# LSTMs over single nodes: the output gate by seven half-size products, and the input sums of every LSTM on GpSimd

## The chip, the cores and the metric

The kernel runs on one core of one Trainium2 chip. The metric is the device time of one execution in microseconds (us). All arithmetic is float32.

## The reference, cut to what matters

A graph network of four layers works on `x` of 128 graphs x 64 nodes x 256 features. Each layer adds its result to `x`. Layers 0, 1 and 3 are not touched. Layer 2 makes two graph mixes and then, for window lengths p = 1 to 4, runs an LSTM over windows of p consecutive nodes and writes its last state over the last node of each window:

```
def step(carry, x_t):
    h, c = carry
    g = x_t @ Wih.T + h @ Whh.T + bias
    i, f, gg, o = jnp.split(g, 4, axis=-1)
    c = sigmoid(f) * c + sigmoid(i) * tanh(gg)
    h = sigmoid(o) * tanh(c)
for p in range(1, MAX_SKIP + 1):
    wins = h[:, :nw * p, :].reshape(Bv * nw, p, Hd)
    last = _lstm_last(Wih[p-1], Whh[p-1], bih[p-1], bhh[p-1], wins)
    h = h.at[:, arange(nw) * p + (p - 1), :].set(last)
```

The state starts at zero, so that for p = 1 (a window is a single node) there is one step, without `h @ Whh.T` and without the gate f: only i, g and o are computed.

## The kernel before

`windows` (line 2150) is the part that computes these LSTMs. The activations lie transposed, features on the 128 partitions in two halves of 128 (index `kc` or `k`), in four tiles `big`, one for every 32 graphs; `nodes(q)` views one as features x node x graph. For each p the windows are cut into chunks: 16 chunks of 16 windows for p = 1, 8 for p = 2, 8 of 10 or 11 windows for p = 3, and 4 of 16 windows for p = 4. Chunks go in pairs, and for every step t of a window `lstm` (line 2239) is called for both chunks of the pair in turn. That makes 72 calls: 16, 16, 24 and 16. A chunk has `W` = 16 x windows columns for each half of its 32 graphs: 256, or 160 and 176 for p = 3.

A gate is a product of a 256 x 256 weight and a 256 x 2W block, two by two blocks of each. Done directly, that is 8 products of 128 x 128 by 128 x W. `lstm` uses Strassen's scheme (in Winograd's form) with 7: sums of weight blocks are made once for each p in `weights` (S1 to S4), sums of the input blocks in each call. The latter stand in the tile `ls_tx`, of which there are two in rotation (`tp`, two buffers): three subtractions, first one of 512 columns (`T[:, 0:2]`), then two of 256 each that need the one before. From the second step on, the same sums of the state h (`S`) are made too, on VectorE.

`gates(xs, fs)` (line 2266) makes the gates `xs` of a call: first (0, 2), the gates i and g together, then o, alone at t = 0 and with f later. `product(m, bank, first)` issues the matmuls of product m for each gate in `xs`; the seven come in the order 1, 6, 7, 5, 2, 4, 3, of which 6, 7, 5 and 4 read `ls_tx`, and 1, 2 and 3 read the activations in `big`. Products of one sum share a PSUM bank, four banks ("a", "b", "f", "d") for each call of `gates`, out of seven in rotation (`lsps`). Around the products VectorE adds partial sums (tiles `ls_z`, `U` in a tile X, and the gate tile `ls_g`) and ScalarE copies (`ls_z`) and applies sigmoid or tanh with the bias. Then VectorE multiplies the gates into c (a tile X), ScalarE takes tanh of c, and VectorE writes the product into `big`.

For p = 1 the gate o is an exception before the change: it is made directly, in two halves of the output, each by two matmuls over 512 columns into one PSUM bank and one sigmoid that reads the bank.

The order of instructions on each engine is set by the framework's scheduler. The engines are called through a wrapper whose line is 799, so that nearly all instructions stand under L799 in the profile and are told apart by their tiles. A matmul in float32 leaves two records in the trace, and so does its weight load.

In the profile the weights of p = 1 and 3 lie in tiles called X, those of p = 2 and 4 in `ls_w` and `ls_s`. GpSimd has 26 instructions before the change, index tables and fills, none in the stage of the LSTMs.

Of the kernel before, what the change touches and what calls it, by code (L numbers as in the profile page):

```python
# [8 lines left out]
F32 = mybir.dt.float32  # L9
I32 = mybir.dt.int32  # L10
AF = mybir.ActivationFunctionType
ALU = mybir.AluOpType
# [1431 lines left out]
P = 128  # L1444
NB = 16
TPB = 4
BT = 512
# [18 lines left out]
class Kernel:  # L1466
# [683 lines left out]
    def windows(self):  # L2150

        nc, o, io = self.nc, self.o, self.io
        cx, (w, wq, gp, tp, zp, psum, pst) = self.stage([("lsw", 1), ("lswq", 1), ("lsg", 2), ("lst", 2), ("lsz", 2),
                                                         ("lsps", 7), ("lstps", 1)], "tile")
        with cx:
            bias = w.tile([P, 4, 8], F32, name="ls_b")
            bh = w.tile([P, 4, 8], F32, name="ls_bh")  # L2160
            with nc.allow_non_contiguous_dma("a few values"):
                nc.sync.dma_start(bias[:], io["L2_gnn_bih"].rearrange("q (k p) -> p q k", p=P))
                nc.sync.dma_start(bh[:], io["L2_gnn_bhh"].rearrange("q (k p) -> p q k", p=P))
            o.add(bias[:], bias[:], bh[:])
            flat = [x[:].rearrange("p t d -> p (t d)") for x in self.X]
            self.c_, self.h_, self.th_ = Ring(flat[12:15]), Ring(flat[8:10]), Ring(flat[10:12])
            self.u_ = Ring([flat[15][:, 0:512], flat[15][:, 512:1024]])
            self.lp = gp, tp, zp, psum, bias

            def load(ap, n, x):  # L2170

                if x is None:
                    return ([wq.tile([P, 4 * D], F32, name=f"ls_w{n}{kc}")[:] for kc in range(2)]
                            + [wq.tile([P, 2 * D], F32, name=f"ls_s{n}{i}")[:] for i in range(3)])
                return [flat[x], flat[x + 1], flat[x + 2][:, 0:512], flat[x + 2][:, 512:1024], flat[x + 3][:, 0:512],
                        flat[x + 3][:, 512:1024]]

            def weights(p):

                out = []  # L2180
                for n, m in enumerate(("Wih", "Whh") if p > 1 else ("Wih",)):
                    t = load(None, n, None if p % 2 == 0 else 4 - 4 * n)
                    ap = io[f"L2_gnn_{m}_t"][p - 1]
                    for kc in range(2):
                        nc.sync.dma_start(t[kc], ap[kc * P:(kc + 1) * P, :])
                    A = [[t[kc].rearrange("p (x k m) -> p x k m", k=2, m=P)[:, :, k, :] for kc in range(2)]
                         for k in range(2)]
                    S1, S2, S4 = (y.rearrange("p (x m) -> p x m", m=P) for y in t[2:5])
                    o.add(S1, A[1][0], A[1][1])
                    o.sub(S2, S1, A[0][0])  # L2190
                    o.sub(S4, A[0][1], S2)
                    S3 = t[5].rearrange("p (x m) -> p x m", m=P) if len(t) > 5 else A[1][0]
                    o.sub(S3, A[0][0], A[1][0])
                    out.append({1: A[0][0], 2: A[0][1], 3: S4, 4: A[1][1], 5: S1, 6: S2, 7: S3,
                                "A": A})
                return out

            ready = weights(1)
            for p in range(1, 5):
                Ws = ready  # L2200
                nw = N // p
                parts = -(-nw // 16)
                chunks = []
                for q in range(NG):
                    w0 = 0
                    for k in range(parts):
                        w1 = w0 + (nw - w0) // (parts - k)
                        chunks.append((q, w0, w1))
                        w0 = w1
                for n in range(0, len(chunks), 2):  # L2210
                    if n == 2 and p < 4:
                        ready = weights(p + 1)
                    if n == 2 and p == 4:
                        self.fetch(0, 8)
                        for i in range(8):
                            self.back(i, pst, "pt")
                    two = [dict(q=q, w0=w0, w1=w1) for q, w0, w1 in chunks[n:n + 2]]
                    for t in range(p):
                        for ch in two:
                            self.lstm(p, t, ch, Ws)  # L2220
            self.fetch(8, NB)
# [17 lines left out]
    def lstm(self, p, t, ch, Ws):  # L2239


        o = self.o
        gp, tp, zp, psum, bias = self.lp
        w0, w1, H = ch["w0"], ch["w1"], self.nodes(ch["q"])
        nw = w1 - w0
        W = nw * 16
        at = slice(t + p * w0, t + p * (w1 - 1) + 1, p)
        node = lambda kc: H[:, kc, at, :]
        half = lambda kc: node(kc).rearrange("p w (h b) -> p h w b", h=2)

        T = tp.tile([P, 4, 256], F32, name="ls_tx")[:, :, 0:W].rearrange("p n (w b) -> p n w b", b=16)
        o.sub(T[:, 0:2], H[:, :, at, 16:32], half(0))
        o.sub(T[:, 2], H[:, 1, at, 16:32], T[:, 0])
        o.sub(T[:, 3], H[:, 1, at, 0:16], T[:, 2])
        parts = [(Ws[0], {1: H[:, 0, at, 0:16], 2: H[:, 1, at, 0:16], 3: H[:, 1, at, 16:32],
                          5: T[:, 0], 7: T[:, 1], 6: T[:, 2], 4: T[:, 3]})]
        if t:
            h = ch["h"].rearrange("p (k h w) -> p k h w", k=2, h=2)
# [6 lines left out]

        def gates(xs, fs):
            G = gp.tile([P, 2, 1024], F32, name="ls_g")
            if p == 1 and len(xs) == 1:
                for k in range(2):
                    ps = psum.tile([P, BT], F32, name="ps")  # L2270
                    for kc in range(2):
                        self.mm(ps[:, 0:2 * W].rearrange("p (w b) -> p w b", b=32), Ws[0]["A"][k][kc][:, xs[0], :],
                                node(kc), kc == 0, kc == 1)
                    self.act(G[:, 0, 2 * W * k:2 * W * (k + 1)].rearrange("p (h w b) -> p h w b", h=2, b=16),
                             ps[:, 0:2 * W].rearrange("p (w h b) -> p h w b", h=2, b=16), fs[0],
                             bias=bias[:, p - 1, 2 * xs[0] + k:2 * xs[0] + k + 1])
                return G
            n = len(xs)
            V = G[:, 0:n, 0:4 * W].rearrange("p x (k h w) -> p x k h w", k=2, h=2)
            banks = {}  # L2280

            def product(m, bank, first):
                if first:
                    banks[bank] = psum.tile([P, 2, 256], F32, name="ps")
                for i, x in enumerate(xs):
                    for j, (A, Bm) in enumerate(parts):
                        out = banks[bank][:, i, 0:W]
                        if len(Bm[m].shape) == 3:
                            out = out.rearrange("p (w b) -> p w b", b=16)
                        self.nc.tensor.matmul(out, A[m][:, x, :], Bm[m], start=first and i == 0 and j == 0,  # L2290
                                              stop=i == n - 1 and j == len(parts) - 1, skip_group_check=True)
                return banks[bank][:, 0:n, 0:W]

            def b(x, k):
                return bias[:, p - 1, 2 * x + k:2 * x + k + 1]

            Z = zp.tile([P, 2, 256], F32, name="ls_z")[:, 0:n, 0:W]
            U = self.u_.next().rearrange("p (x w) -> p x w", x=2)[:, 0:n, 0:W]
            a = product(1, "a", True)
            self.act(Z, a, AF.Copy)  # L2300
            o.add(Z, Z, product(6, "b", True))
            o.add(U, Z, product(7, "f", True))
            o.add(V[:, :, 1, 1], U, product(5, "d", True))
            a = product(2, "a", False)
            for i, x in enumerate(xs):
                self.act(V[:, i, 0, 0], a[:, i], fs[i], bias=b(x, 0))
            o.add(V[:, :, 1, 0], Z, product(4, "f", False))
            for i, x in enumerate(xs):
                self.act(V[:, i, 1], V[:, i, 1], fs[i], bias=b(x, 1))
            o.add(V[:, :, 0, 1], Z, product(3, "d", False))  # L2310
            for i, x in enumerate(xs):
                self.act(V[:, i, 0, 1], V[:, i, 0, 1], fs[i], bias=b(x, 0))
            return G

        s = lambda g, i: g[:, i, 0:4 * W]
        G = gates((0, 2), (AF.Sigmoid, AF.Tanh))
        c = self.c_.next()[:, 0:4 * W]
        o.mul(c, s(G, 0), s(G, 1))
        if t:
            G = gates((3, 1), (AF.Sigmoid, AF.Sigmoid))  # L2320
            o.mul(s(G, 1), s(G, 1), ch["c"])
            o.add(c, c, s(G, 1))
        else:
            G = gates((3,), (AF.Sigmoid,))
# [334 lines left out]
```

## Time and profile before

| | |
|---|---|
| median of 3 runs | 2345.04 us (2342.6 to 2351.49) |
| profiled execution | 2348.6 us, its span 2346.8 us |
| mean granted TensorE clock | 0.993 |
| TensorE matmul busy | 2293.6 us (98%) |
| TensorE weight loads busy | 1629.2 us (69%), beside the matmuls |
| VectorE busy | 1602.6 us (68%) |
| ScalarE busy | 1134.3 us (48%) |
| GpSimd busy | 2.9 us |

Busy times are sums over the profiled execution. Instructions on one engine overlap a little at their ends, so that the distance of two starts is often less than the duration of the first. A view cut to a time window tells what each engine did in a stage; the LSTMs run from about 687 to 1757 us: p = 1 to 838 us, p = 2 to 1108 us, p = 3 to 1416 us, and p = 4 to the end.

### The profile page before, as it was taken

What the parts mean: (1) busy time and instruction counts of PE and PEld (TensorE: products, weight loads), DVE (VectorE), ACT (ScalarE), POOL (GpSimd) and SP (SyncE); (2) the same over time, 40 slices, a digit from 0 to 9 for tenths busy, and PEclk for the clock granted to TensorE, in tenths of its full rate; (3) what the DMA queues carried; (4) which work ended last, traced back from release to release, by engine and by line L of the source; (5) the groups of instructions that cost most, each with busy time, mean ns of one, the idle gap of its engine ahead of it and who ended that gap; (6) DMA issues with size and microseconds to landing.
All of it is one profiled execution on the core that took longest, in us unless ns stands there. A gap on an engine that the chain in (4) does not pass through costs nothing.

```text
span 2346.8 us, 32591 instructions
## 1 busy us (share of the span) xinstructions
PE 2293.6 (98%) x12153; PEld 1629.2 (69%) x12153; DVE 1602.6 (68%) x4006; ACT 1134.3 (48%) x2490; POOL 2.9 (0%) x26
## 2 busy tenths in 40 slices
PE   7999998999999999999999999999999999999989
PEld 4555446986777788888999998888874444444434
DVE  7877676998447777666777667569655566556467
ACT  5665864654436654444444434347445544344321
POOL 0000000000000000000000000000000000000000
PEclk9999999999999999999999999999999999999989
DMA  5000221230010000001000001000020000000001
GB/s 170 1 2 19 64 63 27 73 82 19 1 36 1 1 19 1 1 1 37 1 1 1 1 14 59 1 1 17 1 72 1 1 10 14 14 19 14 15 14 50
DMA packets 61192, 54.86 MB, mean 23 GB/s; under 512 B 15203, under 2 KB 58852, under 8 KB 61028
## 3 DMA queue, kind: packets, MB, share of 16 engines
q1 hardware_dynamic: 61028, 52.73, 7.3%
q8 instruction: 96, 1.57, 0.3%
q14 instruction: 68, 0.56, 0.1%
HBM read 35.93 MB, written 16.78 MB: 22 GB/s over the span
## 4 chain that ended last, share of the span: by engine, by line
PE 80%; DVE 3%; issue 0%; ACT 0%; ACTq 0%; DVEq 0%
PE ps L799 69%; PE acc L799 5%; PE pt L799 4%; PE pe L799 1%; DVE sm_m L799 1%; PE y L799 1%; DVE X L799 1%; DVE aw L799 0%; ACT ls_g L799 0%; DVE ls_g L799 0%; DVE sm_e L799 0%; DVE ls_t L799 0%; DVE XV L799 0%; DVE y L799 0%; DVE n_st L799 0%
## 5 line engine op out<-in xcount | busy, mean ns | idle before, releaser
L799 ACT ACTIVATE ls_g<-ls_g,ls_b 128x512 f32<-128x512 f32 (+4 forms) x472 | 242.9, 565 | 153.2 <-DVE ls_g L799 151.4
L799 ACT ACTIVATE ls_g<-ps,ls_b 128x256 f32<-128x256 f32 (+3 forms) x268 | 115.3, 470 | 330.6 <-PE ps L799 327.3
L799 PE MATMUL ps<-z,w 128*128 128x512 f32 x512 | 259.1, 630 | 0.9 <-ACT z L799 0.9
L799 PE MATMUL ps<-big,X 128*128 128x176 f32 (+3 forms) x848 | 212.9, 366 | 0.8 <-ACT big L799 0.7
L799 DVE TENSOR_TENSOR aw<-at,ed_OST 128x1024 f32<-128x1024 f32 x128 | 150.0, 1220 | 92.7 <-PE ps L799 92.7
L799 DVE TENSOR_TENSOR ls_g<-ls_z,ps 128x512 f32<-128x512 f32 (+5 forms) x256 | 146.9, 579 | 91.4 <-PE ps L799 90.0
L799 PE MATMUL ps<-ls_tx,X 128*128 128x160 f32 (+2 forms) x960 | 207.0, 326 | 0.6 <-ACT ls_g L799 0.6
L799 PE MATMUL ps<-X,X 128*128 128x160 f32 (+1 forms) x896 | 199.1, 306 | 0.0
L799 PE MATMUL ps<-X,ls_w 128*128 128x256 f32 x640 | 190.5, 379 | 0.0
L799 PEld LDWEIGHTS ps<-ls_tx,X 128*128 128x128 f32 x960 | 161.8, 190 | 15.4 <-DVE X L799 5.2
L799 PEld LDWEIGHTS ps<-big,X 128*128 128x128 f32 x848 | 145.9, 190 | 30.6 <-issue 19.4
L799 DVE TENSOR_TENSOR X<-ls_g 128x1024 f32<-128x1024 f32 (+2 forms) x108 | 117.4, 1087 | 51.1 <-ACT ls_g L799 51.1
L799 ACT ACTIVATE r<-ps 128x512 f32<-128x512 f32 x256 | 129.3, 625 | 41.4 <-PE ps L799 41.3
L799 PEld LDWEIGHTS ps<-X,X 128*128 128x128 f32 x896 | 148.4, 190 | 0.0
L799 PE MATMUL ps<-X,ls_s 128*128 128x256 f32 x480 | 142.3, 379 | 0.0
L799 PEld LDWEIGHTS ps<-z,w 128*128 128x128 f32 x512 | 88.8, 193 | 71.1 <-issue 62.6
L799 PE MATMUL ps<-ls_tx,ls_s 128*128 128x256 f32 x464 | 134.7, 379 | 0.0
L799 PE MATMUL ps<-ls_tx,ls_w 128*128 128x256 f32 x464 | 133.3, 380 | 0.0
L799 PEld LDWEIGHTS ps<-X,ls_w 128*128 128x128 f32 x640 | 121.4, 190 | 16.8 <-DVE X L799 0.3
L799 PE MATMUL ps<-big,ls_w 128*128 128x256 f32 x464 | 131.9, 379 | 0.7 <-ACT ls_z L799 0.7
L799 PE MATMUL ps<-ed_S,Q 64*128 64x512 f32 x512 | 128.3, 617 | 0.9 <-DVE XV L799 0.9
L799 ACT ACTIVATE h<-X,n_m,n_r 128x256 f32<-128x256 f32 x192 | 99.6, 589 | 40.9 <-issue 25.0
(532 smaller groups left out, 4012.0 us busy)
## 6 DMA issues: line engine op xcount, KB each, us to landing
X<-in_x_dram SPq DMA_DIRECT2D x32, 512.0 KB
xs<-X SPq DMA_DIRECT2D x16, 512.0 KB
X<-xs SPq DMA_DIRECT2D x16, 512.0 KB
out_dram<-X SPq DMA_DIRECT2D x32, 256.0 KB
X<-in_L_gnn_Wih_t_dram SPq DMA_DIRECT2D x4, 512.0 KB
ls_w<-in_L_gnn_Wih_t_dram SPq DMA_DIRECT2D x4, 512.0 KB
ls_w<-in_L_gnn_Whh_t_dram SPq DMA_DIRECT2D x4, 512.0 KB
w<-in_L_gnn_W_t_dram SPq DMA_DIRECT2D x2, 512.0 KB
```

Of the source, the lines that this page charges most:

```text
L799: i = method(*a, **kw)
```

## The change

For p = 1 the gate o goes through the same seven products as the others (`n` = 1 gate), and the direct form is gone; the weights no longer carry the plain blocks "A" for it. In all 72 calls the three subtractions into `ls_tx` are issued on GpSimd, and not through the ordered wrapper. The sums of the state h stay on VectorE.

```
-                    out.append({1: A[0][0], 2: A[0][1], 3: S4, 4: A[1][1], 5: S1, 6: S2, 7: S3,
-                                "A": A})
+                    out.append({1: A[0][0], 2: A[0][1], 3: S4, 4: A[1][1], 5: S1, 6: S2, 7: S3})
...
         T = tp.tile([P, 4, 256], F32, name="ls_tx")[:, :, 0:W].rearrange("p n (w b) -> p n w b", b=16)
-        o.sub(T[:, 0:2], H[:, :, at, 16:32], half(0))
-        o.sub(T[:, 2], H[:, 1, at, 16:32], T[:, 0])
-        o.sub(T[:, 3], H[:, 1, at, 0:16], T[:, 2])
+        less = lambda y, a, b: self.nc.gpsimd.tensor_tensor(y, a, b, op=ALU.subtract)
+        less(T[:, 0:2], H[:, :, at, 16:32], half(0))
+        less(T[:, 2], H[:, 1, at, 16:32], T[:, 0])
+        less(T[:, 3], H[:, 1, at, 0:16], T[:, 2])
...
         def gates(xs, fs):
             G = gp.tile([P, 2, 1024], F32, name="ls_g")
-            if p == 1 and len(xs) == 1:
-                for k in range(2):
-                    ps = psum.tile([P, BT], F32, name="ps")
-                    for kc in range(2):
-                        self.mm(ps[:, 0:2 * W].rearrange("p (w b) -> p w b", b=32), Ws[0]["A"][k][kc][:, xs[0], :],
-                                node(kc), kc == 0, kc == 1)
-                    self.act(G[:, 0, 2 * W * k:2 * W * (k + 1)].rearrange("p (h w b) -> p h w b", h=2, b=16),
-                             ps[:, 0:2 * W].rearrange("p (w h b) -> p h w b", h=2, b=16), fs[0],
-                             bias=bias[:, p - 1, 2 * xs[0] + k:2 * xs[0] + k + 1])
-                return G
             n = len(xs)
```

## The prediction

> **What bounds the kernel now.** I read the page's busy times first, then the stages of the LSTMs cut to windows, then the order in time of one chunk of p = 1, and last the groups by shape and the list of waits. The window table has, for each stretch, the stretch's length and the busy time of TensorE, its weight loads, VectorE, ScalarE and GpSimd:
>
> ```profile
> 687.00:838.50 151.50, 151.50 (x576) 109.32 (x577) 115.59 (x181) 92.28 (x160) 0.00 (x0) 1.00 0.02 8
> 838.50:1108.00 269.50, 269.50 (x1255) 236.24 (x1254) 182.72 (x294) 118.11 (x220) 0.00 (x0) 1.00 0.04 12
> 1108.00:1416.00 308.00, 307.26 (x2129) 304.38 (x2128) 215.99 (x458) 140.97 (x336) 0.00 (x0) 1.00 0.04 11
> 1416.00:1757.00 341.00, 338.87 (x1579) 291.64 (x1578) 232.95 (x424) 158.78 (x270) 0.00 (x0) 1.00 0.06 18
> ```
>
> TensorE is busy without a break in p = 1 and 2 and idle for 0.74 and 2.13 us in p = 3 and 4, at the full granted clock (1.00). A busy TensorE is not yet one at its pace, so the starts of its records must show that. One chunk of p = 1 in order of time, TensorE rows, then VectorE rows (start, length, row, and in brackets idle time before):
>
> ```profile
> 754.29 2.75 PE L799 MATMUL ps<-ls_tx,X 128*128 128x256 f32 x12
> 756.88 1.89 PE L799 MATMUL ps<-big,X 128*128 128x256 f32 x6
> 758.60 1.03 PE L799 MATMUL ps<-ls_tx,X 128*128 128x256 f32 x4
> 759.47 4.46 PE L799 MATMUL ps<-big,X 128*128 128x256 f32 x14
> 763.77 0.59 PE L799 MATMUL ps<-ls_tx,X 128*128 128x256 f32 x2
> ...
> 753.65 1.23 DVE L799 TENSOR_TENSOR X<-ls_g 128x1024 f32<-128x1024 f32 x1 [0.77 <-ACT ls_g L799]
> 755.43 0.69 DVE L799 TENSOR_TENSOR ls_z<-ls_z,ps 128x512 f32<-128x512 f32 x1 [0.55 <-PE ps L799]
> ...
> 759.67 0.69 DVE L799 TENSOR_TENSOR ls_g<-ls_z,ps 128x512 f32<-128x512 f32 x1 [0.92 <-PE ps L799]
> 760.27 0.69 DVE L799 TENSOR_TENSOR ls_tx<-big 128x512 f32<-128x512 f32 x1
> 760.88 0.68 DVE L799 TENSOR_TENSOR ls_g<-ls_z,ps 128x512 f32<-128x512 f32 x1
> 761.47 0.88 DVE L799 TENSOR_TENSOR ls_tx<-big,ls_tx 128x256 f32<-128x256 f32 x2
> 763.13 1.23 DVE L799 TENSOR_TENSOR X<-ls_g 128x1024 f32<-128x1024 f32 x1 [0.78 <-ACT ls_g L799]
> ```
>
> The first twelve records, all of 256 columns, take 756.88 - 754.29 = 2.59 us, 0.216 us each, with no gap to the next row. The chunk repeats after 763.77 - 754.29 = 9.48 us and has 576/16 = 36 records: 28 of 256 columns (14 matmuls of the gates i and g, two records each) and 8 of 512 (the gate o; the rows name only the first shape). So a record of 512 takes (9.48 - 28 x 0.216)/8 = 0.429 us. These are paces from start to start, and TensorE holds them through p = 1: it sets the time of this stage, and everything else lies beside it. In the same chunk VectorE is idle for 0.55 + 0.10 + 0.92 + 0.78 = 2.35 us (the 0.10 between rows left out here). In the list of waits TensorE waits for another engine six times in the 1070 us of the LSTMs, for 3.2 us in all.
>
> **Part 1: the gate o by seven products.** It takes out 4 matmuls of 512 columns (8 records) in each of the 16 chunks and puts in 7 of 256 (14 records); the order of instructions of the built programs agrees: 48 more matmuls, 3 for each chunk. A chunk goes from 9.48 us to 42 x 0.216 = 9.07 us: 0.41 us less, 16 times, **-6.6 us**. The weight loads rise from 36 to 42 of 0.190 us, 8.0 us in 9.07, still covered. These are the gains on the path, and small because one eighth of the products of one gate in three is saved, in a stage that is 6% of the span.
>
> What it adds beside the path: five VectorE additions of 256 columns in each chunk (before, sigmoid read the bank directly), and on ScalarE two sigmoids of 512 columns from PSUM become one copy and four sigmoids. p = 2 already has calls of just this form at t = 0 (o alone, seven products), so their cost stands in the trace:
>
> ```profile
> 846.50 0.41 DVE L799 TENSOR_TENSOR X<-ls_z,ps 128x256 f32<-128x256 f32 x1
> 846.83 0.68 DVE L799 TENSOR_TENSOR X<-X,X 128x512 f32<-128x512 f32 x1
> 847.43 0.41 DVE L799 TENSOR_TENSOR ls_g<-X,ps 128x256 f32<-128x256 f32 x1
> ```
>
> 0.33 us from start to start where the next is ready, 0.41 us by itself: five take 1.65 to 2.05 us. ScalarE goes from 92.28/16 = 5.8 us a chunk, by about 0.4 + 0.5 + 0.7 + 2 x 0.5 us less 2 x 0.68, to about 6.8 of 9.07. Its waits are not at their limit. The o gate now takes four PSUM banks where it took two, so eight banks of seven in rotation pass in each chunk. The calls of p = 2 at t = 0 pass the same eight, with more on VectorE, and TensorE is busy all through them; I cost this at nothing. If VectorE lagged by more than the bank rotation covers, the next product 1 or 6 would wait for a bank.
>
> **Part 2: the input sums on GpSimd.** VectorE loses 0.61 + 0.88 = 1.49 us in a chunk of p = 1. Its work there goes from 9.48 - 2.35 = 7.13 us to 7.13 - 1.49 + 1.65 to 2.05 = 7.3 to 7.7 us, of 9.07: still not the bound, with 1.4 to 1.8 us spare. Without the move it would be 8.8 to 9.2 us, the chunk itself.
>
> GpSimd makes no such subtraction in this trace. The nearest rows are
>
> ```profile
> L2353 POOL IOTA ed_J<- 128x512 f32 x1 | 0.6, 563 | 374.5 <-DVE bn_sh L799 374.5
> ...
> masks.py:199 POOL TENSOR_SCALAR_AFFINE_SELECT ident<-ident 128x128 f32<-128x128 f32 x1 | 0.3, 297 | 0.0
> ```
>
> Iota only writes: 0.56 us for 512 columns, and half for 256, gives 1.1 us a call, a lower end. The select reads one tensor; less 0.09 us, the cost of GpSimd's one-column fills, it takes 0.205 us for 128 columns, 1.6 ns a column: 0.91 + 2 x 0.50 = 1.9 us a call. Two tensors read in turn would double the slope: 1.73 + 2 x 0.91 = 3.6 us, the upper end. I take 1.9, the only row that reads at all.
>
> Is it on the path? A new wait stands at product 6, for GpSimd in place of VectorE. A tile of sums is free when product 4 of o of the call before last is done; by the order of instructions all 42 records of the other chunk and product 1 (4 records) stand between that and product 6. So GpSimd has 46 x 0.216 = 9.9 us for 1.9 (1.1 to 3.6) at p = 1, and 46 x 0.136 = 6.3 us for smaller sums in the shortest calls of p = 3. Nothing else is queued on GpSimd behind a sum but later sums; the first two can be made when the first activations are final, near 567 us, 120 us before TensorE needs them. Cost: nothing, up to 9.9 us a call.
>
> What the lighter VectorE gives back: between 680 and 1765 us the starts of TensorE's records exceed their paces (0.216, 0.149, 0.136 us by shape), counting single steps more than 30% over, by 9.3 us in all, of which 2.1 at the start of p = 3 (1108 to 1118 us) and 3.3 in p = 4 while finished blocks are turned back (1580 to 1611 us). In and just before these stretches input sums take 1.7 and 2.6 us of VectorE. The rest of the chain there (ScalarE, products into X) stays, so I take a third, **-1.4 us**, of bounds 0 and -9.3.
>
> **The rule against it.** VectorE instructions with two operands in SBUF are 1.23 + 1.29 = 2.5 us of a chunk (c, and the two products into `big`); the additions read PSUM. This trace has no moment where GpSimd reads beside them. The Trainium skill's page "SBUF — State Buffer", section "Who interferes with whom", says that a VectorE instruction with two SBUF inputs contends with a GpSimd instruction that reads SBUF: whichever starts first holds the shared port for its whole length. Its page "GPSIMD Engine Reference", section "Elementwise — side-by-side cycle accounting", keeps VectorE as the rule for elementwise work and gives 4497 ns for a 2048-column addition on GpSimd; my estimate from that is 1.1 + 2 x 0.55 = 2.2 us a call. By the two rules at their worst, every GpSimd instruction holding up VectorE in full, a chunk would be 7.3 to 7.7 + 2.2 = 9.5 to 9.9 us of VectorE, and the p = 1 stage would lose 7 to 13 us of what it gains.
>
> **Sum.** -6.6 - 1.4 = -8.0 us. The profiled execution was 2348.6 us (span 2346.8), 3.6 us above the median of the runs: 2340.6 us against it, **2337.0 us** against the median of 2345.0, or 0.34% less. What is late next is still TensorE.
>
> **Rivals.**
> (a) *VectorE becomes the bound of p = 1 because GpSimd's reads hold up its two-operand instructions.* Three such instructions meet three sums a chunk. With 1.9 us all blocked, VectorE needs 9.2 to 9.6 us: 0.1 to 0.5 us too much, 2 to 8 us in 16 chunks, 2339 to 2345. With 3.6 us all blocked, 10.9 to 11.3 us: 29 to 36 us lost, 2366 to 2373, slower than before. It turns from gain to loss when a chunk is held up 1.8 to 2.2 us in all. Against: they must collide every time, and PSUM's seven banks let VectorE lag. In p = 2 to 4 VectorE is at 68 to 70% with sums of its own, and the loss has room.
> (b) *GpSimd is far slower than its rows say on these strided reads, and the sums come late.* From 9.9 us a call, each us more costs up to 16 us in p = 1 alone. At 12 us: +34, 2371. Nothing in the profile speaks for it but the lack of a row.
> (c) *VectorE was late more often than I credit*: with 5 to 9.3 us of relief the sum is -11.6 to -15.9, 2329 to 2333.
>
> **How the numbers follow.** Half a per cent, 11.7 us, is about what a measurement of this kernel can tell from no change (its three runs spread over 9 us). My forecast, paced by TensorE throughout, 2333 to 2342, gets 0.74; (a) 0.12, of which 0.07 over half a per cent slower; (b) 0.03; (c) 0.11. The range leaves out the far end of (a) and (b) and of (c): 2330 to 2349. Within half a per cent 0.79, faster 0.11, slower 0.10.
>
> **What would show it.** Right: in p = 1 the chunk repeats every 9.07 us with 42 records at 0.216, the stage is near 145 us, GpSimd shows 216 subtractions of about 0.9 and 0.5 us, the waits of TensorE for GpSimd are empty, VectorE's idle time in p = 1 shrinks to 1 to 2 us a chunk, and the later stages keep their lengths within 2 us. Wrong: VectorE's products into X or `big` longer than 1.23 and 0.65 us or starting late while GpSimd runs (a), rows of TensorE waiting for `ls_tx` on POOL (b), or stages p = 3 and 4 shorter by more than 4 us (c).

## The result: 0.31% slower, and the profile after

Over 20 runs of each kernel the median went from 2347.72 to 2354.74 us; the ratio is 1.0031, 95% interval 1.0023 to 1.0039, which is 5 to 9 us slower where 8 us less were forecast. The profiled execution took 2354.23 us, its span 2352.3. The same two stretches of time that were shown of before, now of after:

```profile
687.00:838.50 151.50, 144.61 (x645) 119.05 (x644) 128.36 (x204) 95.05 (x182) 54.94 (x45) 1.00 0.01 4
838.50:1108.00 269.50, 268.57 (x1233) 232.26 (x1232) 169.23 (x251) 118.37 (x220) 50.67 (x48) 1.00 0.02 6
```

TensorE now idles for 6.9 us in a stretch in which it had no idle time. The stages are measured from the first product on `ls_tx` to the first matmul with the weights of p = 2, from there to the first product on `ls_tx` of p = 3, to the first matmul with the weights of p = 4, and to the last product on `ls_tx`. So measured p = 1 takes 157.2 us (before 150.9), p = 2 269.8 (266.9), p = 3 306.3 (306.0) and p = 4 334.5 (334.8). The parts of the program whose code is the same, ahead and behind, were 1.5 and 2.3 us shorter in this execution; in the runs below p = 1 begins anywhere between 681.6 and 690.2 us, so those two say nothing of the change. The loss is in p = 1, and a little in p = 2.

Two neighbouring chunks of p = 1 after the change, rows of TensorE, GpSimd and VectorE from the order in time (start, length, row, idle time before):

```profile
763.77 1.28 POOL L2251 TENSOR_TENSOR ls_tx<-big 128x512 f32<-128x512 f32 x1 [5.94 <-PE ps L799]
...
764.06 2.08 DVE L799 TENSOR_TENSOR X<-ls_g 128x1024 f32<-128x1024 f32 x1
...
765.13 2.41 POOL L2251 TENSOR_TENSOR ls_tx<-big,ls_tx 128x256 f32<-128x256 f32 x2
...
767.34 1.36 DVE L799 TENSOR_TENSOR big<-ls_g 128x512 f32<-128x512 f32 x2 [0.27 <-ACT ls_g L799]
...
767.50 1.46 PE L799 MATMUL ps<-big,X 128*128 128x256 f32 x6
...
768.62 0.67 DVE L799 TENSOR_TENSOR X<-ls_z,ps 128x512 f32<-128x512 f32 x1
...
769.43 1.10 PE L799 MATMUL ps<-ls_tx,X 128*128 128x256 f32 x4 [0.47 <-DVE X L799]
...
773.46 1.23 DVE L799 TENSOR_TENSOR X<-ls_g 128x1024 f32<-128x1024 f32 x1
...
773.82 2.02 POOL L2251 TENSOR_TENSOR ls_tx<-big 128x512 f32<-128x512 f32 x1 [6.27 <-PE ps L799]
...
775.91 1.54 POOL L2251 TENSOR_TENSOR ls_tx<-big,ls_tx 128x256 f32<-128x256 f32 x2
...
776.85 1.75 DVE L799 TENSOR_TENSOR big<-ls_g 128x512 f32<-128x512 f32 x2 [1.49 <-ACT ls_g L799]
```

In the first chunk GpSimd's long subtraction starts at 763.77, VectorE's product into c 0.29 us later, and c takes 2.08 us where it took 1.23. In the second, c starts first (773.46) and keeps its 1.23 us; now it is GpSimd's subtraction, 0.36 us later, that takes 2.02 and not 1.28. Then the sums run on beside the products into `big`, which take 1.75 in place of 1.29. Whoever comes first goes through, the other waits. The Trainium skill's page "SBUF — State Buffer", section "Who interferes with whom", states that a VectorE instruction with two SBUF inputs contends with a GpSimd instruction that reads SBUF, and that the order of issue decides who blocks; this trace agrees, with these numbers. The additions with one operand in PSUM keep their 0.67 to 0.69 us. GpSimd's start is not by chance: its tile of sums is released by the o gate's last product that reads it, just when c is due. So the engines meet in every chunk between 730 and 830 us: in every second one c takes 2.07 or 2.08 us, in the others GpSimd's long subtraction takes 1.95 to 2.02 us and the products into `big` are held up.

A chunk takes 10.01 us, averaged over ten (9.48 before, 9.07 forecast). The second TensorE row (769.43) is where TensorE feels it: product 4 (`ls_tx` x4) waits for VectorE's addition U (`X<-ls_z,ps`, 768.62). In the list of TensorE's waits over all LSTMs (us in total, times, longest) that is a line which was not there before:

```profile
PE ps L799 <- DVE X L799: 7.7, 15, 0.8
```

### The profile page after: what moved, and what is told of

Same layout as the page of the kernel before. It is cut to its first block, busy times and chain, and to the rows that moved or that the text cites. A ratio compares the mean times of both kernels' runs of the same rounds, so it can differ in the third digit from the quotient of the medians.

```text
span 2352.3 us, 33109 instructions
## 1 busy us (share of the span) xinstructions
PE 2289.9 (97%) x12249; PEld 1642.1 (70%) x12249; DVE 1569.6 (67%) x3870; ACT 1141.6 (49%) x2522; POOL 210.1 (9%) x242
## 4 chain that ended last, share of the span: by engine, by line
PE 75%; DVE 6%; ACT 1%; issue 1%; DMA 0%; DVEq 0%; ACTq 0%
PE ps L799 65%; PE acc L799 5%; PE pt L799 4%; DVE X L799 2%; ACT ls_g L799 1%; PE pe L799 1%; DVE sm_m L799 1%; DVE big L799 1%; PE y L799 1%; DVE ls_g L799 1%; DVE aw L799 0%; DVE ls_z L799 0%; DVE sm_e L799 0%; DMA ls_w<-in_L_gnn_Wih_t_dram 0%; DVE ls_s L799 0%
## 5 line engine op out<-in xcount | busy, mean ns | idle before, releaser
L799 ACT ACTIVATE ls_g<-ls_g,ls_b 128x512 f32<-128x512 f32 (+4 forms) x504 | 259.6, 567 | 149.3 <-DVE ls_g L799 146.8
L799 DVE TENSOR_TENSOR ls_g<-ls_z,ps 128x512 f32<-128x512 f32 (+5 forms) x288 | 159.2, 562 | 187.9 <-PE ps L799 187.7
L799 ACT ACTIVATE ls_g<-ps,ls_b 128x256 f32<-128x256 f32 (+2 forms) x252 | 101.0, 442 | 317.5 <-PE ps L799 314.8
L799 PE MATMUL ps<-ls_tx,X 128*128 128x256 f32 (+2 forms) x1088 | 244.1, 335 | 8.1 <-DVE X L799 7.4
L799 PEld LDWEIGHTS ps<-ls_tx,X 128*128 128x128 f32 x1088 | 183.9, 190 | 27.5 <-issue 12.1
L2251 POOL TENSOR_TENSOR ls_tx<-big 128x512 f32<-128x512 f32 (+1 forms) x72 | 99.6, 1384 | 1112.5 <-PE ps L799 912.9
L799 PE MATMUL ps<-big,X 128*128 128x256 f32 (+2 forms) x816 | 184.8, 333 | 0.7 <-ACT big L799 0.7
L799 DVE TENSOR_TENSOR X<-ls_g 128x1024 f32<-128x1024 f32 (+2 forms) x108 | 129.0, 1195 | 47.5 <-ACT ls_g L799 46.6
L799 PEld LDWEIGHTS ps<-big,X 128*128 128x128 f32 x816 | 139.1, 190 | 10.6 <-DVE ls_g L799 1.9
```

Source lines behind the costliest of these rows:

```text
L799: i = method(*a, **kw)
L2251: less = lambda y, a, b: self.nc.gpsimd.tensor_tensor(y, a, b, op=ALU.subtract)
```

## The experiments

Chunk times below are the mean of ten chunks in the middle of p = 1, from the starts of TensorE's records; "held up" is what c and the two products into `big` take beyond 1.22 and 2 x 0.69 us in a chunk. A ratio is the time against the kernel before, run beside it, with its 95% interval in brackets.

**The two halves, the reads taken away, and a bank of its own.** First each part of the change alone:

```
o_alone:     -        less = lambda y, a, b: self.nc.gpsimd.tensor_tensor(y, a, b, op=ALU.subtract)
             +        less = o.sub
sums_alone:  before.py with the three subtractions through `less` on GpSimd, nothing else
```

> The gate o of p = 1 by seven products, the input sums left on VectorE. Theory A (GpSimd's reads hold up VectorE's two-operand instructions, and that lateness reaches TensorE through product 4): without GpSimd p = 1 runs near TensorE's pace, 145 to 147 us where the change has 157, and the whole is 3 to 7 us below the kernel before. Theory B (the seven-product form of o alone makes the loop through VectorE and ScalarE longer than 9.07 us a chunk): p = 1 stays at 155 to 160 us and the whole is 5 to 9 us above before.

Measured: ratio 0.9982 (0.9971 to 0.9994), p = 1 147.8 us, 9.15 us a chunk. The seven products do pay, if little (1.4 to 6.8 us by the interval), VectorE has room for the sums, and theory B is out.

> The input sums on GpSimd in all calls, o of p = 1 direct as before. Theory A: the product into c and the products into the activations last 1.5 to 1.6 us and 0.8 us in p = 1 in place of 1.23 and 0.65; of the some 0.7 us a chunk a part shows, because the direct o leaves more room: p = 1 151 to 158 us, the whole 0 to 7 us above before. Theory B: p = 1 151 us, the whole within 2 us of before.

Measured: ratio 1.0006 (0.9996 to 1.0016); p = 1 151.6 us, and nothing held up: c 1.225, `big` 0.689 us, GpSimd's subtractions 1.29 and 0.73. The groups by shape between 730 and 830 us have

```profile
L799 DVE TENSOR_TENSOR X<-ls_g 128x1024 f32<-128x1024 f32 x10 | 12.3, 1225 | 13.4 <-ACT ls_g L799 13.4
L2252 POOL TENSOR_TENSOR ls_tx<-big,ls_tx 128x256 f32<-128x256 f32 x20 | 14.7, 733 | 1.6
L2252 POOL TENSOR_TENSOR ls_tx<-big 128x512 f32<-128x512 f32 x11 | 14.1, 1286 | 72.2 <-PE ps L799 72.2
```

With the direct o the sums happen to run while VectorE adds from PSUM (in one chunk from 772.04 to 774.95 us; c starts at 774.88). My expectation of a hold-up was wrong, and the point is a useful one: it is the meeting that costs, not the sums. p = 2 took 269.4 us, as in the change.

```
write_only:  +        def less(y, a, b):
             +            self.nc.gpsimd.memset(y, 0.0)
             +            self.nc.gpsimd.memset(y, 1.0)
own_bank:    -            o.add(V[:, :, 1, 0], Z, product(4, "f", False))
             +            o.add(V[:, :, 1, 0], U, product(4, "e", True))      # for p == 1
```

> The change with each of GpSimd's subtractions replaced by two fills of the same columns (the input sums are left out, the products take constants in their place): GpSimd writes the same tiles behind the same waits and reads nothing. Theory A: no hold-up, VectorE's product into c back at 1.23 us, p = 1 near 145 us, the whole 6 to 9 us below before. Theory B: p = 1 near 157 us as in the change, the whole about 7 us above before.

Measured: ratio 0.9969 (0.9956 to 0.9983), p = 1 147.4 us, 9.32 us a chunk. The groups by shape between 730 and 830 us, first of the change, then of this kernel:

```profile
L799 DVE TENSOR_TENSOR X<-ls_g 128x1024 f32<-128x1024 f32 x10 | 16.5, 1650 | 0.0
L2251 POOL TENSOR_TENSOR ls_tx<-big 128x512 f32<-128x512 f32 x10 | 16.4, 1639 | 61.8 <-PE ps L799 49.1 <-ACT ls_g L799 12.7
L799 DVE TENSOR_TENSOR big<-ls_g 128x512 f32<-128x512 f32 x20 | 15.9, 835 | 7.4 <-ACT ls_g L799 7.4
```

```profile
L799 DVE TENSOR_TENSOR X<-ls_g 128x1024 f32<-128x1024 f32 x11 | 13.4, 1222 | 0.0
L799 DVE TENSOR_TENSOR big<-ls_g 128x512 f32<-128x512 f32 x20 | 12.9, 689 | 5.4 <-ACT ls_g L799 5.4
L2252 POOL MEMSET ls_tx<- 128x512 f32 x11 | 5.8, 525 | 79.2 <-PE ps L799 79.2
```

The same tiles written on GpSimd, behind the same waits, hold nothing up: c is back at 1.22 and `big` at 0.69 us. With the kernel later_sums below, whose reads stay and are only moved, this shows that the cost is in reads that meet c and `big`. (The fills, 2 x 0.53 + 4 x 0.31 = 2.3 us a chunk, are a little shorter than the undisturbed subtractions, 2.75.)

> The change, but in p = 1 product 4 goes to a PSUM bank of its own and is added to U (Z plus product 7) and not to Z, so that it no longer waits for VectorE to have read product 7 out of the bank they shared; the sums are equal. Theories A and B alike, if product 4 is the place where the lateness reaches TensorE: p = 1 145 to 148 us, the whole 3 to 8 us below before. If VectorE is simply out of time, or the banks run out (ten pass in a chunk, of seven): 155 us or more, as the change.

Measured: ratio 1.0030 (1.0018 to 1.0041), p = 1 157.8 us, 9.94 us a chunk, held up 0.54 (all of it at `big`). The expectation of 145 to 148 us failed. Product 4 no longer waits for U, and nothing is won: TensorE's weight loads wait instead for VectorE's writes of `ls_g`. The list of waits between 700 and 835 us has

```profile
PEld ps L799 <- DVE ls_g L799: 15.1, 26, 0.9
```

The place where the lateness arrives can be moved; it did not go away.

**Another phase, and dose.** These kept the change and moved or scaled GpSimd's reads:

```
later_sums:  +            if len(self.past) > 2:      # p == 1; self.past: node(1) of each call
             +                self.nc.gpsimd.tensor_copy(T[:, 0, 0, 0:1], self.past[-3][:, 15, 31:32])
sums_twice:  each subtraction of p = 1 issued twice
p1_vector:   +        if p == 1: less = o.sub
p1_gpsimd:   +        if p > 1: less = o.sub
```

> The change, but in p = 1 each call's sums on GpSimd begin with a copy of one column out of the activations that the call before last wrote (into the tile of sums, overwritten at once by the first subtraction), so that they start behind VectorE's products into the activations, some 4.8 us later in the chunk, where VectorE has only additions that read PSUM. Order on the other engines as in the change. Theory A with the collision as its cause: product into c at 1.23 us and into the activations at 0.69 us, p = 1 146 to 149 us in place of 157, the whole 4 to 8 us below the kernel before. If the sums on GpSimd were costly for another reason (their own length, or a later tile), p = 1 stays at 155 us or grows.

Measured: ratio 1.0006 (0.9995 to 1.0017), p = 1 150.6 us, 9.42 us a chunk. Between 730 and 830 us:

```profile
L2255 POOL TENSOR_TENSOR ls_tx<-big 128x512 f32<-128x512 f32 x11 | 14.8, 1349 | 2.9 <-PE ps L799 2.1
L799 DVE TENSOR_TENSOR big<-ls_g 128x512 f32<-128x512 f32 x21 | 13.6, 688 | 7.3 <-ACT ls_g L799 7.2
L799 DVE TENSOR_TENSOR X<-ls_g 128x1024 f32<-128x1024 f32 x11 | 13.4, 1222 | 0.0
```

The same reads, started behind the products into `big`: nothing is held up, and 0.59 of the 0.94 us a chunk that the change loses against 9.07 are back. The gain over before that I expected did not come, for two reasons: 9.42 is not 9.07, and p = 2, with 269.7 us, keeps its loss.

> The change with each of the three subtractions of p = 1 issued twice on GpSimd, the second over the first. Theory A: GpSimd reads for twice as long, some 5.5 to 6 us of a chunk, and meets c and both products into the activations in every chunk: c 1.6 to 2.1 us, those 0.9 to 1.1 us each, p = 1 160 to 172 us in place of 157. Theory B: GpSimd's length does not matter as long as the sums are in time (9.9 us): 157 us.

Measured: 2364.6 us in one run, p = 1 164.6 us, 10.49 a chunk; c 1.65 and `big` 1.08 us, held up 1.20. TensorE also waited for the sums themselves here (12.3 us of weight loads between 730 and 830), so part of it is lateness of the tile, and the row of this kernel in the table below counts for less.

> The change with the input sums of p = 1 back on VectorE, those of p = 2 to 4 on GpSimd. Theory A: p = 1 as in the kernel with the gate o alone, 147 to 149 us; p = 2 stays at 269 to 270 us if what it lost (266.9 to 269.8) is GpSimd's reads in its own calls, and returns to 267 if it was handed on by p = 1; p = 3 and 4 306 and 334.5.

> The change with the input sums on GpSimd in p = 1 alone, those of p = 2 to 4 on VectorE. Theory A: p = 1 157 us as in the change; p = 2 back at 267 us if its own GpSimd reads cost the 2 to 3 us, 269 to 270 if p = 1 hands them on.

Measured, one run each: p1_vector 2345.59 us, p = 1 148.4 and p = 2 269.9; p1_gpsimd 2352.81 us, p = 1 156.9 and p = 2 267.0. The 2.9 us of p = 2 come from GpSimd's sums in its own calls. They are not all reads: in write_only, with fills in their place, p = 2 still takes 268.1 us, 1.2 more than before. In p = 3 and 4 both ways take the same within 0.6 us.

**Which way it reaches TensorE.** From the chain of rows above I made theory C: U stands behind the products into `big` on VectorE, these behind tanh of c, and that behind c. write_later and no_tanh should have cut it; o_alone_write_later has the order of write_later without GpSimd's sums, and later_sums_own_bank asks what is left without a hold-up:

```
write_later:          the products into big issued after the next chunk's
                      o.add(V[:, :, 1, 1], U, product(5, "d", True))
o_alone_write_later:  the same, with less = o.sub
no_tanh:              o.mul(half(k), y(0, k), <c>) for p == 1
later_sums_own_bank:  later_sums and own_bank together
```

> The change, but in p = 1 VectorE's products into the activations are issued in the next chunk behind its additions of products 7 and 5 (U and the first write of the gate tile), not ahead of them; GpSimd's sums as in the change. Theory C, made from the runs so far: what GpSimd's reads hold up reaches TensorE through VectorE's order, since U stands behind the products into the activations, these wait for tanh of c, and c is the product that is held up; product 4 cannot overwrite its bank before U. Then p = 1 returns to 146 to 149 us (9.1 to 9.3 a chunk, 10.0 in the change) although c stays held up at 1.4 us or more, and the whole is 1 to 5 us below the kernel before (p = 2 keeps its 2.8 us). If VectorE simply has too little time for the hold-ups, p = 1 stays near 157.

Measured: ratio 1.0011 (1.0001 to 1.0022), p = 1 152.3 us, 9.68 us a chunk. Better than the change, short of what theory C asked; c was no longer held up (1.23), `big` was (0.89).

> The gate o by seven products with all input sums on VectorE, and the products into the activations of p = 1 behind the additions of products 7 and 5 of the next chunk. Theory C: a chunk takes 9.07 to 9.15 us, p = 1 146 to 148 us, the whole 4 to 7 us below before: the best version if VectorE's load, 8.8 of 9.07 us, leaves anything.

Measured: ratio 0.9982 (0.9969 to 0.9994), p = 1 145.9 us, 9.15 us a chunk. p = 1 is 1.9 us shorter than in o_alone, p = 2 1.0 longer (268.5 against 267.5); as a whole it is no better than o_alone.

> The change, but for p = 1 the products into the activations take c and not tanh of c (tanh is still computed and left unused), so that the chain from c to U is 1.06 us and two hand-overs shorter, GpSimd's sums as in the change. Theory C: the chunk falls from 10.0 to 9.1 to 9.4 us. If VectorE has too little time, it stays at 9.8 to 10.

Measured: 2351.19 us in one run, p = 1 151.3 us, 9.59 us a chunk: short of the expectation too.

> The sums started behind the products into the activations, and product 4 of p = 1 in a bank of its own. Without hold-ups 9.4 us a chunk were left of which 9.07 is TensorE's pace. If the wait of product 4 for U makes the rest: 9.1 to 9.2 us a chunk, p = 1 146 to 148 us. If it is another wait on VectorE's queue (product 3 for the addition of product 5): 9.3 to 9.5 us.

Measured: 2345.01 us in one run, p = 1 150.4 us, 9.39 us a chunk: taking away the wait of product 4 for U wins nothing here either.

Side by side, with VectorE's busy time in a chunk:

| | held up | chunk | chunk less held up | VectorE busy | VectorE idle |
|---|---|---|---|---|---|
| the change | 0.72 | 10.01 | 9.29 | 8.33 | 1.68 |
| sums_twice | 1.20 | 10.49 | 9.29 | 8.80 | 1.69 |
| own_bank | 0.54 | 9.94 | 9.40 | 8.08 | 1.86 |
| write_later | 0.40 | 9.68 | 9.28 | 7.84 | 1.84 |
| no_tanh | 0.32 | 9.59 | 9.27 | 7.75 | 1.84 |
| write_only | 0 | 9.32 | 9.32 | 7.62 | 1.70 |
| later_sums | 0 | 9.42 | 9.42 | 7.64 | 1.78 |
| later_sums_own_bank | 0 | 9.39 | 9.39 | 7.53 | 1.86 |
| o_alone | 0 | 9.15 | 9.15 | 8.63 | 0.52 |
| o_alone_write_later | 0 | 9.15 | 9.15 | 8.74 | 0.41 |

Each us held up lengthens the chunk by about a us, whatever the order: with the sums off VectorE a chunk is 9.27 to 9.42 us and the hold-up on top. By this table write_later and no_tanh were faster because the engines met less; that a chain was cut, theory C's particular way, is not shown. What the table shows is that VectorE's idle time in these kernels stays at 1.7 to 1.9 us and takes up none of the hold-up, while with the sums on VectorE it falls to 0.4 to 0.5 in a shorter chunk. The windows from 730 to 830 us of the change, then of o_alone, say the same (TensorE, its loads, VectorE, ScalarE, GpSimd):

```profile
730.00:830.00 100.00, 94.72 (x421) 77.50 (x420) 83.11 (x131) 62.22 (x120) 36.70 (x30) 1.00 0.00 1
```

```profile
730.00:830.00 100.00, 100.00 (x461) 86.12 (x460) 94.34 (x176) 66.16 (x132) 0.00 (x0) 1.00 0.00 1
```

VectorE at 94% goes with the faster kernel, VectorE at 83% with the slower. So VectorE was not out of time in the change; its idle time consists of waits for TensorE's and ScalarE's next result, in rows that stand in order. The sums on VectorE fitted into those waits and cost next to nothing: 9.15 us a chunk, where TensorE's pace is 9.07.

Why a chunk without them is 9.3 to 9.4 and not 9.07 or 9.15 can be read off in part. In write_only two neighbouring chunks take 18.63 us where the pace makes 18.14, and the starts of TensorE's records show where: six steps are 0.07 to 0.10 us longer than 0.216, 0.50 in all, five of them at product 4, which waits for U, and one at product 3, which waits for the addition of product 5. Two of the rows between:

```profile
770.84 0.42 DVE L799 TENSOR_TENSOR X<-ls_z,ps 128x256 f32<-128x256 f32 x1
771.31 0.30 PEld L799 LDWEIGHTS ps<-ls_tx,X 128*128 128x128 f32 x2 [0.31 <-DVE X L799]
```

The same reading of the change, 20.22 us for two chunks from 773.04 us on, finds 2.1 us beyond the pace at these two products, 1.59 of it in the first step of product 4 of the gates i and g. What makes U late without a hold-up was not settled: other orders of the rows and a bank of its own left the 9.3 to 9.4 as they were.

The version to keep is o_alone, 0.9982 of before: seven products for o and no work on GpSimd.

## Why the prediction was wrong, by its own steps

**Part 1 held, less a little.** 42 records at 0.216 us make 9.07 us; o_alone has 9.15. Of the -6.6 us, the middle chunks would give (9.48 - 9.15) x 16 = 5.3, but the stage as a whole got 150.9 - 147.8 = 3.1 us shorter; the ratio of o_alone, 0.9982, is 4 us. What the prediction puts on ScalarE is wrong in two small points that cost nothing: the gate o takes one copy and three sigmoids, not four, and its terms add up to 7.0 us and not 6.8; in o_alone ScalarE was busy for 66.16 of 100 us, 6.1 a chunk.

**Part 2 held in what it looked at.** The sums were not late in the change: no matmul waited for them, and weight loads four times in all LSTMs, for 1.2 us together. They took 1.28 and 0.74 us undisturbed at p = 1, and 3.7 us a call with the hold-ups, of 9.9 available. My 1.9 us a call, from the select's row, was too low; the undisturbed 1.29 + 2 x 0.73 = 2.75 lies between my ends of 1.1 and 3.6. The slope, (1.29 - 0.73)/256 = 2.2 ns a column, agrees with the Trainium skill's page "GPSIMD Engine Reference", section "Elementwise — side-by-side cycle accounting" (4497 ns for an addition of 2048 columns). My estimate from it, 2.2 us a call, left out some 0.17 us that each of the three subtractions takes on top of its columns (1.29 - 512 x 0.0022).

**The step that failed is in rival (a)**: "It turns from gain to loss when a chunk is held up 1.8 to 2.2 us in all". I had taken VectorE's 1.4 to 1.8 us of idle time in a chunk as slack that must first be used up, so the sum has nothing for a hold-up. It was no slack: 0.72 us held up cost 0.69 (10.01 against write_only's 9.32), 16 x 0.69 = 11 us by the middle chunks and 157.2 - 147.4 = 9.8 by the stage. And "they must collide every time" was held against it; they do, since the event that frees the tile of sums fixes the phase. The right price of (a) was the hold-up itself.

**The thin margin stood in the profile of before.** I read TensorE's waits and found few. Its weight loads wait too, and the list of waits of p = 1 before the change has

```profile
PEld ps L799 <- issue: 22.5, 94, 0.2
PEld ps L799 <- DVE X L799: 4.2, 15, 0.7
```

The second line, fifteen waits in sixteen chunks, names VectorE's U, but most of them were not waits for U. Thirteen of the fifteen gaps are 0.24 us, as long as the 94 of the first line, which stand before loads behind a record of 512 columns; there U had ended 0.10 to 0.22 us before the load began. Only two loads, with gaps of 0.69 and 0.38 us, began 0.05 us behind U's end. One chunk, with product 4 itself at 758.60 in the rows shown ahead:

```profile
757.28 0.68 DVE L799 TENSOR_TENSOR X<-ls_z,ps 128x512 f32<-128x512 f32 x1
758.18 0.19 PEld L799 LDWEIGHTS ps<-ls_tx,X 128*128 128x128 f32 x1 [0.24 <-DVE X L799]
```

U ends at 757.96. So in a chunk in which VectorE idles for 2.35 us, its result U was ready only 0.22 us before the load of product 4, which adds into a bank that VectorE must read first, and 0.64 us before the matmul. I treated PSUM as seven banks in rotation and missed that inside a call a bank is used twice. It is this margin, and not the idle time, that should have been held against a hold-up of 0.72 us; how much of it the new order of the gate o leaves, the profile of before does not tell.

**The relief did not come.** I credited -1.4 us to the lighter VectorE in p = 2 to 4. p = 3 and 4 changed by +0.3 and -0.3 us, and p = 2 lost 2.9.

The sum over p = 1: forecast 150.9 - 6.6 = 144.3 us, measured 157.2, 12.9 more: 9.8 for the reads, and 3.1 that write_only, with 147.4, has without them. With 2.9 of p = 2 and 1.4 of relief that is 17.2 us; the unchanged parts were 3.7 us shorter in the profiled execution, which leaves the 13.5 between -8.0 and the +5.5 of the two spans.

## What to carry to other kernels

Idle time of an engine is slack only where nobody waits for its next result. Before pricing a delay at nothing, look at how long each result lies ready before it is used, and for banks or tiles that are used twice inside a step; and compare a wait that a profile names with the end of what it names. Here work that filled the waits of VectorE cost 0.08 us a chunk (9.15 against 9.07), and moving it away gained nothing. Before elementwise work goes to GpSimd, see which of VectorE's instructions have both operands in SBUF and whether the event that starts GpSimd's work fixes them to the same moment.

## What was not expected of the hardware

A hold-up goes both ways and depends on who starts first: c 2.08 us in place of 1.23 when GpSimd was 0.29 us ahead, GpSimd's subtraction 2.02 in place of 1.28 when c was 0.36 us ahead. GpSimd's fills of the same tile held nothing up (c 1.222, `big` 0.689 us), nor did its subtractions beside additions that read PSUM (0.688 us). A copy of a single column on GpSimd took 0.51 us in later_sums, while a fill of one column takes 0.09, so a small instruction there need not be a cheap one.
